# A 7x7 depthwise convolution on TensorE: from 32x4 output tiles with three products to paired 8x8 tiles with two products each

## The chip, the cores and the metric

The kernel runs on one core of one Trainium2 chip. The metric is the device time of one execution in microseconds, as the median of several runs. All data are float32. TensorE (PE) multiplies, with a separate weight-load stream (PEld); VectorE (DVE), ScalarE (ACT) and GpSimd (POOL) do the rest on chip; SyncE (SP), ACT and POOL also issue DMAs.

## The reference, cut to what matters

The input is an image `x` of 384 channels, 192 by 192. Layer 0 is a transposed-attention block: group norm, a 1x1 convolution to q, k and v with 2x2 max pooling, a 3x3 depthwise convolution, attention over channels, GELU, nearest upsampling and a projection; its output is added to `x`. Layer 1 is the stage that this change concerns:

```python
def _L1_conv_ref(x, weight):
    w_sym = (weight + rot90(weight, 1) + rot90(weight, 2) + rot90(weight, 3)) * 0.25
    return _dwconv(x, w_sym, 1, 3)      # 7x7, one filter per channel, padding 3

x = x + _L0_conv_ref(_gn(x), ...)       # layer 0
x = x + _L1_conv_ref(_gn(x), weight)    # layer 1; _gn: mean and variance over 12 channels
```

So the last stage normalises the image by group, convolves each channel with its own symmetrised 7x7 filter with zero padding, and adds the unnormalised image.

## The kernel before, in words

The kernel is one program whose stages follow each other: statistics of `x`; the q and k stage, in blocks of image rows (`products`, `pooled`, `depthwise`); the v stage with attention and projection (`convolve`, `depthwise_v`, `attend`, `project`, `residual`); and the 7x7 stage. Most of the order on each engine is written out by hand: `keep` pins an instruction to its program order.

**How a depthwise convolution becomes a product.** For one channel, an output tile of some rows and columns is a vector on the output partitions; the input window under it is a vector on the contracted partitions; the 7x7 filter, spread into a banded matrix, is the stationary operand; and all tiles of the image are the moving columns. Before, a tile is 32 rows (`TR`) by 4 columns (`CP`), 128 outputs, and the image has 6 by 48 = 288 such tiles (`NT`, `NJ`). The window of 38 rows by 10 columns does not fit into 128 partitions, so a channel takes three products of 288 columns: two from `main` (the tile's 32 rows, at two column shifts), and one from `aux`, which holds what is left over: three halo rows above, three below, and two columns of the tile's rows.

**Data in DRAM.** `residual` forms layer 0's result in an on-chip tile `sx` (POOL issues its stores) and writes it to `sd`, laid out by (column in tile, row in tile) so that a load gives `main` directly, and a second time, shifted, to `sh` for the halo rows. The spread filters are built on POOL during the q and k stage by `weights`, in 21 pieces, and written to `wt` (for `main`) and `wh` (for `aux`).

**The 7x7 stage** runs 48 steps of 8 channels (`CB`). In step n:

- ACT's queue issues the loads for step n+2 into three rotating buffers: `w` and `h` (weights), `main` and `aux` (data). The first two steps are loaded from SP's queue.
- POOL does `borders(n+1)`: it adds the mean outside the image (`mm`, `mb`), so that normalisation can be folded into weights and an offset row (`ONE`), and copies 32 rows of `main` into `aux`; then `spread(n-1)` reorders results into rows (`res`) and SP stores them.
- PE computes two channels into one of four PSUM tiles `pc` (`sums`). Each is drained, with the scale `rb`, by four instructions of 32 partitions by 576 elements into `apart`, on DVE and ACT in turn.
- After the second pair, `middle(n+1)` on DVE adds the identity (for the residual, scaled by `sb`) into the weights, and ACT copies the left-over rows (`rest`) and weight columns (`columns`) for step n+1.

Of the kernel before, what the change touches and what calls it, by code (L numbers as in the profile page):

```python
# [8 lines left out]
F32 = mybir.dt.float32  # L9
AF = mybir.ActivationFunctionType  # L10
ALU = mybir.AluOpType
AX = mybir.AxisListType

P = 128
# [47 lines left out]
CP = 4  # L62
NJ = HW // CP
JP = NJ + 2
RUN = NT * JP
HALO = KS // 2
NQ = CP + KS - 1
LEAD = JP + 2


TOP = 32
BOT = 64
ONE = TOP + HALO * NQ
REST = 96
SHR = REST - TOP
GQ = 3 * CP + 1
GR = 6
# [5 lines left out]
CB = 8  # L83


@with_exitstack
def conv_preact_d2(
# [27 lines left out]
    sd = dram.tile([CP * TR, C, RUN], F32, name="sd")  # L115

    sh = dram.tile([SHR, C, RUN], F32, name="sh")

    wt = dram.tile([P, C, 2 * P], F32, name="wt")
    wh = dram.tile([SHR, C, P], F32, name="wh")  # L120
# [143 lines left out]
    z = parkp.tile([P, RUN + 4 * P], F32, name="z")  # L264
    nc.vector.memset(z[:, 0:RUN], 1.0)
    nc.vector.memset(z[:, RUN:], 0.0)
# [338 lines left out]
    with ExitStack() as bx:  # L605
# [6 lines left out]
        def weights(kt, i0, i1):  # L612

            g = gwp.tile([P, GR, GQ, TR], F32, name=f"g{kt}_{i0}", tag="g")
            keep(nc.gpsimd.memset(g, 0.0))  # L620
            for kr in range(KS):
                lo, hi = max(i0, kr), min(i1, kr + TR)
                if lo < hi:
                    keep(nc.gpsimd.tensor_copy(
                        bass.AP(
                            g.tensor,
                            g.offset + ((lo - i0) * GQ + CP - 1) * TR + lo - kr,
                            [g.ap[0], [TR, KS], [GQ * TR + 1, hi - lo]],
                        ),
                        w7s[:, kt, kr, :].unsqueeze(2).to_broadcast([P, KS, hi - lo]),  # L630
                    ))
            yield
            lo, hi = max(i0, HALO), min(i1, HALO + TR)
            cs = slice(kt * P, (kt + 1) * P)
            for v in range(CP if lo < hi else 0):
                keep(nc.gpsimd.dma_start(
                    wt[v * TR + lo - HALO : v * TR + hi - HALO, cs].rearrange("f c n -> c f n"),
                    bass.AP(
                        g.tensor,
                        g.offset + ((lo - i0) * GQ + v) * TR,  # L640
                        [g.ap[0], [GQ * TR, hi - lo], [1, 2 * P]],
                    ),
                ))
            for i in range(i0, i1):
                if HALO <= i < HALO + TR:
                    continue
                f = i * NQ if i < HALO else BOT - TOP + (i - HALO - TR) * NQ
                keep(nc.gpsimd.dma_start(
                    wh[f : f + NQ, cs].rearrange("f c n -> c f n"),
                    bass.AP(  # L650
                        g.tensor,
                        g.offset + (i - i0) * GQ * TR,
                        [g.ap[0], [TR, NQ], [1, P]],
                    ),
                ))

        pieces = [
            (kt, i0, min(i0 + GR, TR + 2 * HALO))
            for kt in range(KT)
            for i0 in range(0, TR + 2 * HALO, GR)  # L660
        ]
        with tc.issue_after(loaded):
            for kt in range(KT):
                cs = slice(kt * P, (kt + 1) * P)
                for f in (ONE, BOT + HALO * NQ):
                    nc.sync.dma_start(
                        wh[f - TOP : f - TOP + 2, cs].rearrange("f c n -> c f n"),
                        z[:, RUN : RUN + 2 * P].rearrange("p (f n) -> p f n", f=2),
                    )
                    for k in range(2):  # L670
                        one = f + k == ONE
                        nc.sync.dma_start(
                            sh[f + k - TOP, cs], z[:, 0:RUN] if one else z[:, RUN : 2 * RUN]
                        )


# [93 lines left out]
        Q = 32  # L770

# [18 lines left out]
        def products(b, sides):  # L790
# [18 lines left out]
            grams, z[:, RUN : RUN + P], z[:, RUN : RUN + grams.shape[1]], start=True, stop=False,  # L809
# [154 lines left out]
        def weights_of(b):  # L964
            return weights(*pieces[b]) if b < len(pieces) else iter(())

# [76 lines left out]
        for b in range(2):  # L1043
# [25 lines left out]
            if b == 0:  # L1069
                with tc.issue_after(stats0):  # L1070
                    for _ in weights_of(b):
                        pass
# [37 lines left out]
        loose = iter(())  # L1110
# [8 lines left out]
        for n, (b, pair, half) in enumerate(groups):  # L1119
# [3 lines left out]
            if s == 0:  # L1123
                if b + 1 < NB:
                    xbs[b + 1] = load_x(b + 1, "xq")
                loose = weights_of(b - 1)
# [109 lines left out]
        early = gwp.tile([P, GR * GQ * TR], F32, name="vb_early", tag="g")  # L1236
# [195 lines left out]
    for i in range(3):  # L1432
        t = sxp.tile([P, LEAD + CP * RB * RUN + LEAD], F32, name=f"sx{i}")
        nc.gpsimd.memset(t, 0.0)
        sxs.append(t)

    junk = wq[:, 0:2, 0 : RB * NT * NJ].rearrange("p k (n j) -> p k n j", j=NJ)
# [21 lines left out]
    sdv = sd.rearrange("(v r) c n -> r c v n", v=CP)  # L1459
# [5 lines left out]
    def project(i, ot, gl, pin=lambda ins: ins):  # L1465
        b = order[i % NBC]
        y = yp.tile([P, NT, NJ, 2], F32, name=f"y{b}_{ot}", tag="y")
# [28 lines left out]
    def residual(i, ot, y, xr, pin):  # L1496
# [3 lines left out]
        xq = xr.rearrange("p t (a j e) -> p a t j e", a=RB, e=CP)  # L1500

        def at(e):

            return LEAD + (e + CP - 1) % CP * RB * RUN + int(e > 0)


        for e, f in ((1, 2), (0, 3)):
            for a in range(RB):
# [3 lines left out]
                            flat.tensor, flat.offset + at(e) + a * RUN,  # L1512
                            [flat.ap[0], [JP, NT], [1, NJ], [at(f) - at(e), 2]],
                        ),
                        xq[:, a, :, :, e : f + 1 : f - e],
# [12 lines left out]
        for k, (e, f) in enumerate(((1, 2), (3, 0))):  # L1528
            pin(
                nc.scalar.activation(  # L1530
                    junk,
                    bass.AP(
                        flat.tensor, flat.offset + at(e),
                        [flat.ap[0], [at(f) - at(e), 2], [JP, RB * NT], [1, NJ]],
                    ),
                    AF.Square, bias=negmid[:, ot : ot + 1], accum_out=sqsum[:, ot, b, k : k + 1],
                )
            )
            if k == 0:
                yield  # L1540
        cs = slice(ot * P, (ot + 1) * P)

        def rows_of(a, nv, shift):
            o = LEAD + a * RUN + shift
            return bass.AP(
                flat.tensor, flat.offset + o, [flat.ap[0], [RB * RUN, nv], [1, RUN]]
            )

        for a in range(RB):
            r = b * RB + a  # L1550
            nc.gpsimd.dma_start(sdv[r, cs], rows_of(a, CP, 0))  # L1551

            halos = []
            if r >= TR - HALO:
                halos.append(((r - TR + HALO) * NQ, -JP))
            if r < HALO:
                halos.append((BOT - TOP + r * NQ, JP))
            for h, shift in halos:
                for q in range(0, NQ, CP):
                    nv = min(CP, NQ - q)  # L1560
                    nc.gpsimd.dma_start(
                        sh[h + q : h + q + nv, cs].rearrange("f c n -> c f n"),
                        rows_of(a, nv, shift + q // CP),
                    )

# [71 lines left out]
    with ExitStack() as ex_:  # L1637

        fixed = ex_.enter_context(tc.tile_pool(name="fixed", bufs=1))
        wbufs = [fixed.tile([P, CB, 2 * P], F32, name=f"w_{i}") for i in range(3)]  # L1640
        early = ex_.enter_context(tc.tile_pool(name="early", bufs=1))
        hbufs = [early.tile([P, CB, P], F32, name=f"h_{i}") for i in range(3)]
        wide = ex_.enter_context(tc.tile_pool(name="wide", bufs=1))
        data = [P, CB, NT, JP]
        auxs, mainbufs = [
            [(wide if i > last else early).tile(data, F32, name=f"{name}{i}") for i in range(3)]
            for name, last in (("aux", 1), ("main", 0))
        ]
        outp = ex_.enter_context(tc.tile_pool(name="outp", bufs=2))

        CENTRE = (CP - 1) * TR
        eye = wide.tile([P, P], F32, name="eye")
        for k in range(CP):
            nc.gpsimd.tensor_copy(
                eye[:, k * TR : (k + 1) * TR], ident[:, (CP - 1 - k) * TR : (CP - k) * TR]
            )
# [10 lines left out]


        for h in hbufs:
            nc.gpsimd.memset(h[0:TR, :, 2 * TR :], 0.0)  # L1670
            nc.gpsimd.memset(h[REST:P, :, TR:], 0.0)

        def load_w(n):
            w = wbufs[n % len(wbufs)]
            queue(n)(w, wt[:, span(n)])
            return w

        def load_h(n):
            h = hbufs[n % len(hbufs)]
            queue(n)(h[TOP:REST], wh[:, span(n)])  # L1680
            return h

        def columns(n):

            k = 2 * TR
            w, h = ws[n]
            keep(nc.scalar.copy(h[0:TR, :, 0 : 2 * TR], w[k : k + TR, :, 6 * TR :]))
# [328 lines left out]
```

## Time and profile before

| | |
|---|---|
| median of 3 runs | 2701.74 us (2700.86 to 2702.03) |
| profiled execution, time | 2689.47 us |
| its span | 2687.8 us |
| mean granted TensorE clock | 0.986 |
| 7x7 stage, first to last product | 2109.6 to 2677.0 us |
| busy over the span: PE, DVE, ACT, POOL | 93%, 84%, 53%, 54% |

The profile is one execution, whose own time is 12.3 us under the median of the other runs; durations are taken from it. A group's row names the line of the kernel, the engine, the operation, output and inputs, and shape and count; then busy time, mean length of one, and idle time of the engine before them with what ended it. PE's instructions overlap, so their spacing is read from starts and not from lengths; an f32 product shows as two instructions, each with a weight load.

### The profile page before, as it was taken

Reading aid. Unit: us, or ns where it says so; the run is one execution under the profiler, and the core shown is the slowest. Engines: PE = TensorE matmul, PEld = TensorE weight load, DVE = VectorE, ACT = ScalarE, POOL = GpSimd, SP = SyncE. Lnnn points to the kernel's source line nnn. Section 1 sums busy time; section 2 is a strip of 40 time slices with the busy share of each in tenths; the row PEclk is TensorE's granted clock in tenths of the full one; section 3 lists DMA queues with packets and bytes.
Section 4 is the critical chain, followed back from the end, with each engine's and each line's share of the span. In section 5 each row is a group of like instructions: output and inputs, shape, how many; then the busy total and the mean of one; then the engine's idle time right before and its main releaser. Section 6 shows DMA issues by size and latency. Waiting matters only on the chain. (4 is left out here: it accounts for less than half of the span.)

```text
span 2687.8 us, 29574 instructions
## 1 busy us (share of the span) xinstructions
PE 2509.0 (93%) x8893; PEld 1628.8 (61%) x8893; DVE 2270.1 (84%) x3172; ACT 1420.9 (53%) x2711; POOL 1462.9 (54%) x1587
## 2 busy tenths in 40 slices
PE   0298999999999999999899999999999799999998
PEld 0144565656565656565565666666666577777776
DVE  7986788888888888878699989998888788899887
ACT  0032667676767676776213223222234677777776
POOL 1013788888887988876212311001011677878876
PEclk9999999999999999999899999999999899999999
DMA  9962354546363645443428997657657999999998
GB/s 378 399 248 53 106 177 118 157 117 189 109 191 84 181 124 170 131 119 70 127 89 307 387 359 234 230 180 255 208 164 249 339 352 360 374 367 372 363 380 255
DMA packets 467630, 609.59 MB, mean 227 GB/s; under 512 B 250224, under 2 KB 399312, under 8 KB 450704
## 3 DMA queue, kind: packets, MB, share of 16 engines
q1 hardware_dynamic: 407104, 311.83, 37.0%
q0 software_dynamic: 37344, 148.84, 15.4%
q10 hardware_dynamic: 23024, 147.05, 14.6%
q8 instruction: 71, 1.16, 0.2%
q14 instruction: 87, 0.71, 0.1%
HBM read 370.93 MB, written 208.21 MB: 215 GB/s over the span
## 5 line engine op out<-in xcount | busy, mean ns | idle before, releaser
L563 PE MATMUL pv<-xv,wq 128*128 128x384 f32 x1512 | 498.0, 490 | 13.9 <-DVE rows L569 6.2
L1920 PE MATMUL pc<-main,w 128*128 128x288 f32 x1536 | 435.3, 406 | 4.0 <-POOL aux L1840 1.2
L563 PEld LDWEIGHTS pv<-xv,wq 128*128 128x128 f32 x1512 | 289.1, 192 | 214.3 <-DVE rows L569 6.9
L1940 DVE TENSOR_SCALAR apart<-pc,rb 32x576 f32<-32x576 f32 x384 | 312.2, 813 | 75.2 <-PE pc L1920 56.0
L897 POOL TENSOR_TENSOR qk<-qk,more 128x384 f32<-128x384 f32 x290 | 309.7, 1074 | 109.9 <-ACT more L896 100.9
L1938 ACT ACTIVATE apart<-pc,rb 32x576 f32<-32x576 f32 x384 | 281.4, 733 | 132.2 <-PE pc L1920 127.5
L1920 PEld LDWEIGHTS pc<-main,w 128*128 128x128 f32 x1536 | 289.3, 189 | 89.0 <-PE pc L1920 3.9
L1551 POOL DMA_DIRECT2D sd<-sx x96 | 72.4, 757 | 493.0 <-DVE sx L1510 474.4
L596 DVE SCALAR_TENSOR_TENSOR vb<-rows,wd,vb 128x576 f32<-128x576 f32 x360 | 293.8, 818 | 10.7
L897 POOL TENSOR_TENSOR qk<-qk,rows 128x384 f32<-128x384 f32 x216 | 230.5, 1072 | 76.2 <-ACT rows L896 69.9
L1920 PE MATMUL pc<-aux,h 128*128 128x288 f32 x768 | 248.6, 406 | 0.7 <-POOL main L1828 0.4
L929 DVE SCALAR_TENSOR_TENSOR bank_r<-ring,wd,bank_r 128x384 f32<-128x384 f32 x383 | 236.4, 617 | 6.8
L1879 POOL COPY res<-apart 128x1152 f32<-128x1152 f32 (+1 forms) x96 | 223.5, 2355 | 11.5 <-ACT apart L1938 6.2
L1037 PE MATMUL bank_b<-rows,more 128*128 128x384 f32 x528 | 220.4, 499 | 2.0 <-ACT bank_c L1139 1.2
L1510 DVE TENSOR_TENSOR sx<-xr,y 128x576 f32<-128x576 f32 x180 | 203.9, 1173 | 18.1 <-ACT y L1481 15.1
L1117 DVE TENSOR_TENSOR rows<-bank_c,rows 128x384 f32<-128x384 f32 x132 | 73.3, 555 | 126.7 <-PE bank_c L1037 68.6
L569 DVE TENSOR_REDUCE rows<-pv 128x192 f32<-128x768 f32 x144 | 137.6, 956 | 49.8 <-PE pv L563 49.8
L1763 DVE SCALAR_TENSOR_TENSOR w<-eye,sb,w 128x512 f32<-128x512 f32 x96 | 175.9, 1871 | 1.5
L1530 ACT ACTIVATE wq<-sx,negmid 128x1152 f32<-128x1152 f32 x96 | 120.6, 1256 | 102.6 <-DVE sx L1510 100.4
L1920 PEld LDWEIGHTS pc<-aux,h 128*128 128x128 f32 x768 | 144.5, 189 | 43.6 <-POOL main L1828 2.5
L896 ACT ACTIVATE more<-ring,wd 128x384 f32<-128x384 f32 x290 | 170.3, 608 | 0.0
L1456 ACT ACTIVATE gl<-po 128x288 f32<-128x288 f32 x96 | 39.5, 411 | 225.2 <-PE po L1449 225.2
(349 smaller groups left out, 4934.7 us busy)
## 6 DMA issues: line engine op xcount, KB each, us to landing
sd<-sx POOLq DMA_DIRECT2D x96, 600.0 KB, 9.9
out_dram<-res SPq DMA_DIRECT2D x192, 288.0 KB, 11.0
main<-sd ACTq DMA_DIRECT2D x46, 1200.0 KB, 6.7
xr<-in_x_dram SPq DMA_DIRECT2D x45, 1152.0 KB, 12.3
xq<-in_x_dram SPq DMA_DIRECT2D x21, 2304.0 KB, 8.6
xv<-in_x_dram SPq DMA_DIRECT2D x126, 384.0 KB, 7.3
w<-wt ACTq DMA_DIRECT2D x46, 1024.0 KB, 7.2
xs<-in_x_dram SPq DMA_DIRECT2D x24, 1536.0 KB, 15.2
```

The costliest lines, as they stand in the source:

```text
L563: nc.tensor.matmul(ps[:, u, 0 : RB * HW], wq[:, kt, o : o + P], xb[:, u, kt, :], start=(kt == 0), stop=(kt == KT - 1),)
L596: pin(nc.vector.scalar_tensor_tensor(dst, src, w, dst, ALU.mult, ALU.add))
L896: keep(nc.scalar.mul(part.rearrange("p (h w) -> p h w", w=PS), src, w))
L897: keep(nc.gpsimd.tensor_tensor(flat, flat, part, ALU.add))
L929: nc.vector.scalar_tensor_tensor(into, src, w, before, ALU.mult, ALU.add)
L1037: nc.tensor.matmul(ps[:, 0:HN], lhs, rhs, start=start, stop=True, skip_group_check=True)
L1510: nc.vector.tensor_tensor(bass.AP(flat.tensor, flat.offset + at(e) + a * RUN, [flat.ap[0], [JP, NT], [1, NJ], [at(f) - at(e), 2]],), xq[:, ...
L1763: nc.vector.scalar_tensor_tensor(mid, eye.unsqueeze(1).to_broadcast([P, 4, P]), sb[:, c : c + 1], mid, ALU.mult, ALU.add,)
L1879: keep(copy(res[ps, k], apart[ps, :, k].rearrange("p e n -> p n e")))
L1920: nc.tensor.matmul(ahead[q][:, k, 0 : NT * NJ], lhs, rhs, start=(j == 0), stop=(j == 2), skip_group_check=True,)
L1938: keep(nc.scalar.mul(dst, src, scale))
L1940: keep(nc.vector.tensor_scalar_mul(dst, src, scale))
```

## The change

A tile becomes 8 rows by 8 columns (`ED`), 64 outputs; the image has 24 by 24 = 576 of them, in two halves of 288. The window is 14 rows by 16 columns, taken as two products of 14 rows by 8 columns at two column shifts, plus an offset row. For each channel and shift, one half of the tiles goes to PSUM partitions 0 to 63 and the other to 64 to 127, with the same 64-column weights: four products per channel. There is no `aux`, no `h`, no `sh` and no `wh`.

- `main` has 25 slots (`SLOTS`) of 25 tiles. Two DMAs of 32 partitions load eight image rows per slot; `below` copies the lower rows of the window on chip from the slots of the next strip: 32 partitions on POOL, 24 on ACT, two instructions each.
- `borders` works on the two loaded 32-partition blocks only: the two end columns, and one slot above and one below the image.
- A PSUM tile of two channels is drained by one instruction of 128 partitions by 576 elements, three of four on ACT, the fourth on DVE. `apart` now collects 16 channels.
- `swapped` turns results with VectorE's 32x32 transposes, six of 768 elements per 16 channels, one after each drain of the next two steps; `stored` writes runs of four image rows, 24 DMAs per 16 channels.
- `middle` adds into four places of 128 elements instead of two of 512, on 96 partitions.
- `weights` builds three tiles instead of 21 pieces; each is written by 28 DMAs in runs of 64 elements. `residual` writes eight column phases: four DMAs of 150 to 175 element runs per row pair and channel tile, and no halo copies.

The core of the diff:

```diff
-CP = 4
-NJ = HW // CP
-JP = NJ + 2
-RUN = NT * JP
+ED = 8
+NJ = HW // ED
+JP = NJ + 1
+STRIPS = NT * JP
+SLOTS = 4 * NT + 1
+RUN = SLOTS * JP
...
-    sd = dram.tile([CP * TR, C, RUN], F32, name="sd")
-    sh = dram.tile([SHR, C, RUN], F32, name="sh")
-    wt = dram.tile([P, C, 2 * P], F32, name="wt")
-    wh = dram.tile([SHR, C, P], F32, name="wh")
+    sd = dram.tile([ED * ED, C, RUN], F32, name="sd")
+    wt = dram.tile([2, P, C, ED * ED], F32, name="wt")
...
         def load_main(n):
             main = mainbufs[n % len(mainbufs)]
-            queue(n)(main.rearrange("p c t j -> p c (t j)"), sd[:, span(n)])
+            for k in range(2):
+                queue(n)(
+                    main[2 * k * Q : (2 * k + 1) * Q].rearrange("p c t j -> p c (t j)"),
+                    sd[k * Q : (k + 1) * Q, span(n)],
+                )
             return main
...
+        def below(n, copy, base, rows, cs=slice(0, CB)):
+            main = mains[n]
+            to = main[base + Q : base + Q + rows, cs].rearrange("p c t j -> p c (t j)")
+            src = main[base : base + rows, cs].rearrange("p c t j -> p c (t j)")
+            keep(copy(to[:, :, 0 : 2 * STRIPS], src[:, :, STRIPS : 3 * STRIPS]))
...
+        def swapped(n, apart):
+            res = outp.tile([P, NT, RQ, HW], F32, name=f"res{n}", tag="res")
+            for k in range(NT):
+                keep(
+                    nc.vector.transpose(
+                        res[:, k].rearrange("p r (j q) -> p j r q", q=ED)[:, :, ::-1],
+                        apart[:, k].rearrange("p c (s j) -> p j (c s)", j=NJ),
+                    )
+                )
+                if k % 3 == 2:
+                    stored(n, res, k // 3)
+                yield
...
+            for q in range(CB // 2):
+                ps = pc.tile([P, 2, 512], F32, name=f"pc{n}_{q}", tag="pc")
                 for k in range(2):
                     i = 2 * q + k
+                    for j in range(2):
+                        rows = ONE + 1 - j
+                        for h in range(2):
+                            keep(
+                                nc.tensor.matmul(
+                                    ps[h * 2 * Q : (h + 1) * 2 * Q, k, 0 : 2 * NT * NJ],
+                                    w[0:rows, j, i],
+                                    main[0:rows, i, 2 * NT * h : 2 * NT * (h + 1), j : j + NJ],
+                                    start=(j == 0), stop=(j == 1), skip_group_check=True,
+                                )
                             )
...
+                if q == 3:
+                    keep(nc.vector.tensor_scalar_mul(dst, src, rb[:, c : c + 1]))
+                else:
+                    keep(nc.scalar.mul(dst, src, rb[:, c : c + 1]))
+                next(swapping, None)
+                if q == 0 and n + 1 < steps:
                     middle(n + 1)
+                    below(n + 1, nc.scalar.copy, 2 * Q, KS * ED - Q)
```

## The prediction

> **What bounds the kernel now.** I first read the table by stretches of time, because the edit concerns one stage. Its columns are the stretch, its length, then busy time and instruction count of PE, PEld, DVE, ACT and POOL, the granted clock, the DMA share and GB/s.
>
> ```profile
> 2000.00:2100.00 100.00, 81.49 (x309) 59.95 (x307) 87.79 (x109) 51.59 (x114) 19.82 (x30) 0.90 0.68 238
> 2300.00:2400.00 100.00, 99.65 (x411) 77.13 (x410) 86.99 (x86) 77.03 (x95) 78.40 (x78) 1.00 1.02 368
> ```
>
> Inside the 7x7 stage (second line) TensorE never stops and the DMA engines are full as well; the other three engines run at 77 to 87%. The groups (busy us, mean ns of one, idle before) give the price list:
>
> ```profile
> L1920 PE MATMUL pc<-main,w 128*128 128x288 f32 x1536 | 435.3, 406 | 4.0 <-POOL aux L1840 1.2 <-issue 1.1 <-POOL main L1828 0.9
> L1940 DVE TENSOR_SCALAR apart<-pc,rb 32x576 f32<-32x576 f32 x384 | 312.2, 813 | 75.2 <-PE pc L1920 56.0 <-POOL aux L1840 6.8 <-POOL aux L1848 6.8
> L1938 ACT ACTIVATE apart<-pc,rb 32x576 f32<-32x576 f32 x384 | 281.4, 733 | 132.2 <-PE pc L1920 127.5
> L1867 ACT COPY aux<-main 32x2304 f32<-32x2304 f32 x48 | 101.7, 2119 | 0.6
> L1840 POOL COPY aux<-main 32x2304 f32<-32x2304 f32 x48 | 101.0, 2104 | 3.0
> ```
>
> PE waits 4 us in all for the stage's main products, while DVE and ACT wait for PE: PE is the bound. Its pace is read from the timeline (start, length, count), at the same place in two successive channels:
>
> ```profile
> 2305.50 0.65 PE L1920 MATMUL pc<-aux,h 128*128 128x288 f32 x2
> 2306.96 0.65 PE L1920 MATMUL pc<-aux,h 128*128 128x288 f32 x2
> ```
>
> 1.46 us for a channel of three products. Each f32 product is two instructions, so a slot is 1.455/6 = 242.5 ns; the 406 ns is the length of one instruction, overlapping the next. A step of 8 channels is 11.64 us, 48 steps 559 us. The stage's products run from 2109.6 to 2677.0 us: 567 us, 11.82 a step.
>
> How near DMA is to taking over is seen in its queues over 2200 to 2500 us (packets, MB, share) and in a wait:
>
> ```profile
> q10 hardware_dynamic: 11527, 81.11, 72.1%
> q1 hardware_dynamic: 39176, 28.89, 29.2%
> POOL main L1828 <- DMA main<-sd: 86.0, 38, 4.9
> ```
>
> q10 (loads) moves 81.11/(0.721 x 300) = 375 GB/s while it has the engines, q1 (stores in 768-byte runs) 330. The loads come just in time, so bytes matter as much as products.
>
> [...] LDWEIGHTS time goes by columns. [...] 163 ns for 96 columns, 190 for 128. [...] min/median/max below, where the minimum fell beside an idle POOL. [...]
>
> ```profile
> L1763 DVE SCALAR_TENSOR_TENSOR w<-eye,sb,w x96: 736/2080/2739, 2107.2 to 2662.2; 128x512 f32<-128x512 f32 x96
> ```
>
> Two more rows of the trace before price operations that the change adds: the transposes of an earlier stage (same columns), and a run of weight loads with tiny products (a row of the groups by shape).
>
> ```profile
> L861 DVE STREAM_TRANSPOSE turns<-qk x144: 534/578/579, 202.8 to 1296.7; 128x384 f32<-128x384 f32 x144
> ```
>
> ```profile
> L489 PEld LDWEIGHTS bank_y<-mean,wq 128*128 128x128 f32 x54 | 6.3, 192 | 0.5 <-issue 0.5
> ```
>
> **The change part by part, per step of 8 channels.**
>
> PE: three products of 128 output columns become four of 64, in two column halves, all with 288 moving columns. In program order each half issues its two passes (h0 h0 h1 h1 h0 ...). A half's second pass waits for its first, but can run beside the other half's first, so a steady stream has two in flight: 8 instructions in 4 slots, 0.97 us a channel, 7.76 us a step. Without overlap: 8 slots, 15.52 us. Issue allows it: in the L489 row 54 weight loads with their one-column products take 6.3 us, 117 ns a pair, so two pairs need at most 234 of a slot's 242 ns.
>
> ACT: three drains of 576 elements per partition (733 each, whatever the partitions) = 2.20; two lower-row copies of 2400 elements, by L1867 2.2 each = 4.4; three DMA issues (before, 0.34 for w and a median of 0.61 for main) = 1.5. Sum 8.1 us. Gone are five drains, the L1867 copy, the two h copies and two issues.
>
> POOL: two border additions of 400 elements; from L1828 (325 ns at 48, 395 at 96) 1.46 ns an element, 0.84 each; two row copies of 200, 0.35 each (L1855: 507 for 384); two lower-row copies at L1840's rate, 2.2 each. Sum 6.8 us. The res copies (two of 2358) and the aux work go.
>
> DVE: one drain 0.81; four additions into w of 128 elements, 736 less 384 elements at 1.04 ns = 0.34 each, 1.4; three transposes of 768 elements, from L861's 578 at 384 0.98 each, 2.9. Sum 5.1 us. [...] median less minimum of L1763 is 1.34 us; if each of the four pays that, 10.5 us.
>
> SP: 12 stores instead of 4, each issue 0.316 us by the old ones: 3.8 us. It runs nothing else there.
>
> DMA: loads fall from 1200+1024+600+256 KB to 1250 (64 of 128 rows are loaded, the rest copied) + 512 KB, 1.80 MB; stores stay 1.18 MB, in runs of 3072 bytes. At 375 GB/s for both, 7.9 us; at the 398 GB/s seen from 70 to 135 us with long runs, 7.5. [...]
>
> The buffer ring is the last term. A main buffer's load is queued on ACT when the products three steps back end (about 1 us), lands in 6.7 to 15.2 us (say 8.5), then borders 2.4, copies 4.4, products 7.8: 24.1 us over three buffers, 8.0 a step; at 10.5 us landing 8.7.
>
> New waits: ACT's lower-row copies wait for POOL's border work on the same buffer, and behind them in ACT's queue stand two drains and the next step's DMA issues; the additions into w can wait for POOL on DVE, with a transpose and the fourth drain behind, which PE needs four PSUM tiles later; SP's stores wait for transposes, with only stores behind them.
>
> Five resources thus lie between 6.8 and 8.1 us with little slack, and they wait for one another, ACT's late DMA issue above all. I take 8.6 us; bounds 8.0 (ACT, DMA) and 10.5. So 48 x 8.6 = 413 against 567: **-154 us**.
>
> Stage ends. Start: the first product waits for borders, then 600-element copies (0.75 us each) for two channels only, and 1800-element ones for the rest; the last stores of ot 0 take four POOL issues of 0.75 instead of two before main can load. Removed: h memsets 3.7 us on POOL, hidden. I take +4 (0 to +8). End: after the last drain six transposes (5.9) and 12 issues (3.8) stand where 2.2 us copies and four issues stood: +4 (+2 to +7).
>
> Earlier stages. The padding-weight building drops 21 memsets of 2.2 us and about 130 small copies from POOL for three of each; its DMAs stay near 80 at about 0.9 us but in 256-byte runs. PE is 99.8% busy there (600 to 900 us), so 0; if slower packets delay loads, +5. In the projection stage 192 stores to sd replace 96 and the 54 halo stores, 72+40 us of issue becoming 145 on POOL, which is 9 to 16% busy: 0. The residual addition (L1510, 1172 ns for 576) gets other strides; I keep its price. Bounds 0.97 and 1.36 us; only the 45 at the stage's DVE-bound end (first line above: DVE 88, PE 81) lie on the path, -9 to +9.
>
> Sum: -154 + 4 + 4 = -146. The profiled execution took 2689.5 us (span 2687.8); the median of three is 2701.7, 12 above it. Carried over: **2556 us**.
>
> **Rivals.**
> A. The halves do not overlap (f32 passes, or weight loads into the other half held back). Then 15.52 us a step, 745 + 9 against 567, plus 8: about 2896, slower. It decides once a channel's eight instructions need more than 1.48 us, 6.1 slots, i.e. under half the possible overlap. For it: nothing here shows two tiles at once. Against: [...] L489's issue pace.
> B. [...] four short additions behind 2.2 us POOL copies, 10.5 us a step: 504 - 567 + 8 = -55, 2647. For: L1763's median. Against: POOL is idle a fifth of the time[...].
> C. [...] For: POOL already waits 86 us for main. Against: stores run between.
>
> **How the numbers follow.** Forecast (8.0 to 10 us a step) 0.62: own range 2515 to 2625. B and C together 0.18: 2600 to 2700. A, whole or mostly, 0.18: above 2707. No change 0.02; about 0.2% (5 us) is what this measurement can tell. Faster 0.80, slower 0.18. The range 2510 to 2720 leaves out A and a little below.
>
> **What would show it.** PE's products in pairs a few ns apart and 7.8 to 8.6 us a step; busy ACT near 6.6 us a step, POOL near 6.8; transposes near 0.98 us; DMA still near full at 30% fewer bytes. Starts 242 ns apart, never together, mean A; additions into w of over 1.3 us with PE waiting for DVE mean B; main landing after 10 us or more with POOL waiting for it mean C.

## The result, and the profile after

The changed kernel takes 2881.4 us (median of 4; before 2701.9 in the same comparison): **1.0665 times the time before, 95% interval 1.0646 to 1.0683**. The forecast was faster.

The table by stretches (columns as before: length, then PE, PEld, DVE, ACT, POOL, granted clock, DMA share, GB/s) now reads:

```profile
2000.00:2100.00 100.00, 74.16 (x291) 54.56 (x290) 79.90 (x89) 50.03 (x112) 34.71 (x48) 0.88 0.90 195
2300.00:2400.00 100.00, 65.59 (x405) 37.95 (x404) 73.42 (x51) 43.98 (x34) 45.07 (x41) 0.84 0.77 195
```

In the 7x7 stage (second line) nothing is full any more: PE 66%, DVE 73%, ACT and POOL under half, DMA 0.77 at 195 GB/s where it was 1.02 at 368. Engines that all have slack in a stage that got longer point to waits of engines for one another. The stage's products run from 2132.4 to 2851.1 us: 15.0 us a step against 11.8. Of the 190 us between the two profiled spans, 152 are the stage, 23 its later start, 15 what follows the last product.

The groups of the page give the prices to set beside the forecast's (busy, mean ns | idle before, what ended most of it):

```profile
L1848 PE MATMUL pc<-main,w 120*64 120x288 f32 (+1 forms) x3072 | 503.9, 475 | 222.1 <-ACT main L1779 120.0
L1814 DVE STREAM_TRANSPOSE res<-apart 128x768 f32<-128x768 f32 x144 | 293.4, 2061 | 117.5 <-DMA main<-sd 44.4
L1862 ACT ACTIVATE apart<-pc,rb 128x576 f32<-128x576 f32 x144 | 101.5, 738 | 413.4 <-DMA out_dram<-res 139.4
L1761 POOL TENSOR_TENSOR main<-main,mm 32x400 f32<-32x400 f32 x95 | 88.1, 928 | 392.0 <-DMA main<-sd 341.2
L1694 DVE SCALAR_TENSOR_TENSOR w<-eye,sb,w 96x128 f32<-96x128 f32 x192 | 221.8, 1212 | 5.7 <-DMA w<-wt 5.7
```

PE, which before waited under 5 us for its products in all (4.0 for those from `main`, 0.7 for those from `aux`), waits 222; a transpose takes 2061 ns where 980 were forecast; drains and border additions cost what was forecast. The odd entry is the third: ACT's **drain**, which needs only PE's products and a free buffer, waits for the landing of a **store**. One step on the timeline shows how (start, length, engine, count, idle before and its end):

```profile
2398.28 0.38 ACTq L1624 DMA_DIRECT2D w<-wt  x1
...
2398.71 7.84 ACTq L1624 DMA_DIRECT2D main<-sd  x2
...
2406.65 0.74 ACT L1862 ACTIVATE apart<-pc,rb 128x576 f32<-128x576 f32 x1 [9.19 <-DMA out_dram<-res]
...
2407.41 2.20 ACT L1779 COPY main<-main 24x2400 f32<-24x2400 f32 x1
...
2409.52 2.19 ACT L1782 COPY main<-main 24x2400 f32<-24x2400 f32 x1
2409.71 0.67 PE L1848 MATMUL pc<-main,w 121*64 121x288 f32 x2 [3.05 <-ACT main L1779]
```

ACT's queue issues three loads for a later step. The first issue takes 0.4 us; the pair after it 7.8, since the second of the pair is held. Behind it, in ACT's order, stand a drain and both lower-row copies, and for these copies PE waits. What holds the issue is seen in the semaphores of the trace, on which it records waits and landings. SP's and ACT's DMAs share eight, in turn: each of the eight has 222 or 223 of the 1780, and from 2180 to 2640 us SP's 360 stores leave out 90 places of the turn, as many as ACT issues loads. An issue waits until the DMA eight places earlier has landed: on the four semaphores whose landings the trace has in full, each of 886 issues ends 0.33 us or more after that landing. Here the second load of `main` goes out at 2406.21 us, 0.07 us after the landing, at 2406.14, of a store that SP had issued at 2400.31 on the same semaphore. Before, a step had four stores and four loads, so a load always met the semaphore of an older load (ACT's loads stand on four of the eight, SP's stores on the other four). Now it has twelve stores and three loads, and a load meets a store's, or that of the weight load issued just ahead. The stores in turn wait for the slow transposes (last line below). The waits between 2135 us and the end sum it up (engine, line waited for, us, times, longest):

```profile
POOL main L1761 <- DMA main<-sd: 324.5, 75, 10.2
...
ACT apart L1862 <- DMA out_dram<-res: 139.4, 15, 10.3
ACT apart L1862 <- DMA w<-wt: 133.2, 15, 9.8
PE pc L1848 <- ACT main L1779: 120.0, 34, 6.6
...
SPq L1798 <- DVE res L1814: 232.5, 71, 25.6
```

The DMA queues over 2200 to 2500 us (packets, MB, share) show a second loss:

```profile
q10 hardware_dynamic: 7328, 35.77, 47.9%
q1 hardware_dynamic: 11237, 23.02, 30.2%
```

Loads move 35.77/(0.479 x 300) = 249 GB/s while they hold the engines, against 375 before. A 20000-byte packet of `main` takes a median of 1407 ns in the trace after 2135 us, 14.2 GB/s an engine.

Finally, rival A named nearly this time (2896), but not for its reason. One step's products, on the timeline of PE:

```profile
2304.33 7.98 PE L1848 MATMUL pc<-main,w 121*64 121x288 f32 x62 [1.47 <-ACT main L1782]
```

These are 62 of the step's 64 instructions, two a product (the first two ran at 2302.19 us, ahead of a wait), with a median length of 406 ns. Their starts follow one another by some 40 and some 205 ns in turn, so a pair takes 0.243 us and 64 take 7.8, as forecast. In series they would need 15.5. At 2302.19 us the two instructions of one product, alone on PE, start 265 ns apart; at 2304.33 one of each half start 7 ns apart. The halves do overlap; PE then stands idle, and the mean granted clock of the stretch is 0.84 where it was 1.00. That clock costs too: an instruction took 406 ns at the median where the granted clock was 1.0, and 687 where it was 0.5. Over the whole stage the mean is 475 ns, and PE is busy 10.5 us a step at a mean clock of 0.83, where f15 below has 410 ns and 8.1 us at 0.99. How much of the longer stage is this clock and how much the waits, no run separates.

### The profile page after: what moved, and what is told of

It is laid out like the page before. It is cut to its first block, busy times and chain, and to the rows that moved or that the text cites. A ratio compares the mean times of both kernels' runs of the same rounds, so it can differ in the third digit from the quotient of the medians.

```text
span 2877.7 us, 30797 instructions
## 1 busy us (share of the span) xinstructions
PE 2443.9 (85%) x9661; PEld 1497.1 (52%) x9661; DVE 2303.8 (80%) x3068; ACT 1294.4 (45%) x2424; POOL 1317.6 (46%) x1329
## 3 DMA queue, kind: packets, MB, share of 16 engines
q10 hardware_dynamic: 19344, 84.97, 11.9%
## 5 line engine op out<-in xcount | busy, mean ns | idle before, releaser
L1848 PE MATMUL pc<-main,w 120*64 120x288 f32 (+1 forms) x3072 | 503.9, 475 | 222.1 <-ACT main L1779 120.0
L1848 PEld LDWEIGHTS pc<-main,w 120*64 120x64 f32 (+1 forms) x3072 | 304.6, 160 | 420.7 <-issue 282.3
L1512 POOL DMA_DIRECT2D sd<-sx x192 | 143.9, 753 | 540.4 <-DVE sx L1475 497.3
L1814 DVE STREAM_TRANSPOSE res<-apart 128x768 f32<-128x768 f32 x144 | 293.4, 2061 | 117.5 <-DMA main<-sd 44.4
L599 DVE SCALAR_TENSOR_TENSOR vb<-rows,wd,vb 128x576 f32<-128x576 f32 x360 | 293.6, 817 | 10.6
L1862 ACT ACTIVATE apart<-pc,rb 128x576 f32<-128x576 f32 x144 | 101.5, 738 | 413.4 <-DMA out_dram<-res 139.4
L1761 POOL TENSOR_TENSOR main<-main,mm 32x400 f32<-32x400 f32 x95 | 88.1, 928 | 392.0 <-DMA main<-sd 341.2
L1694 DVE SCALAR_TENSOR_TENSOR w<-eye,sb,w 96x128 f32<-96x128 f32 x192 | 221.8, 1212 | 5.7 <-DMA w<-wt 5.7
L1010 PE MATMUL bank_x<-xq,wq 128*128 128x384 f32 x378 | 154.7, 491 | 1.0 <-ACT bank_b L1062 1.0
L1010 PE MATMUL bank_y<-xq,wq 128*128 128x384 f32 x378 | 155.0, 492 | 0.0
L1444 PE MATMUL pr<-gl,wp 128*128 128x288 f32 x576 | 142.6, 406 | 0.0
## 6 DMA issues: line engine op xcount, KB each, us to landing
xs<-in_x_dram SPq DMA_DIRECT2D x24, 1536.0 KB, 15.5
```

The source lines that it names most:

```text
L599: pin(nc.vector.scalar_tensor_tensor(dst, src, w, dst, ALU.mult, ALU.add))
L1010: nc.tensor.matmul(ps[:, 0:HN], lhs, rhs, start=start, stop=True, skip_group_check=True)
L1444: nc.tensor.matmul(ps[:, 0:H], wp[:, ct, ot * P : (ot + 1) * P], gl[:, ct, h * H : (h + 1) * H], start=(ct == 0), stop=(ct == KT - 1),)
L1512: nc.gpsimd.dma_start(sdv[r + a, cs, RQ - e : ED - e, o : o + n], bass.AP(flat.tensor, flat.offset + JP + (a * ED + e) * STRIPS - (e > 0) ...
L1694: nc.vector.scalar_tensor_tensor(mid, eye[0 : 3 * Q, k].rearrange("p r q -> p (r q)").unsqueeze(1).to_broadcast([3 * Q, 4, ED * RQ]), sb[0 ...
L1814: nc.vector.transpose(res[:, k].rearrange("p r (j q) -> p j r q", q=ED)[:, :, ::-1], apart[:, k].rearrange("p c (s j) -> p j (c s)", j=NJ),)
```

## The experiments

Three suspects from the trace: **S**, the loads' semaphores are coupled to the stores'; **T**, the transposes take 2.06 us; **L**, loads of 32 partitions run at two thirds of the old rate. Per kernel: ratio to before, us a step from first to last product start, and us from the last product start to the end of the span.

| kernel | edit against the change | ratio (95%) | a step | end |
|---|---|---|---|---|
| before | | 1 | 11.8 | 11 |
| after | | 1.0665 (1.0646-1.0683) | 15.0 | 27 |
| e2_flat | T out | 1.0394 (1.0342-1.0446) | 13.8 | 24 |
| e3_swload | S out | 1.0107 (1.0070-1.0143) | 11.9 | 32 |
| e4_mid | one load of 64 partitions | 1.0053 (1.0040-1.0066) | 11.8 | 25 |
| e12_mid_two | same place, two loads of 32 | 1.0693 (1.0672-1.0713) | 15.0 | 27 |
| e5_mid_sw | S, L out | 0.9919 (0.9904-0.9934) | 10.6 | 33 |
| e9_mid_sw_flat | S, L, T out | 0.9868 (0.9840-0.9896) | 10.3 | 37 |
| e11_mid_sw_po | S, L, T out, result in order | 0.9863 (0.9842-0.9883) | 10.1 | 37 |
| f13_po_r3 | e11, three result buffers | 0.9837 (0.9805-0.9869) | 9.8 | 53 |
| f14_po_half | e11, stores of half the bytes | 0.9690 (0.9657-0.9723) | 9.4 | 38 |
| f15_po_six | e11, half the stores | 0.9467 (0.9439-0.9496) | 8.6 | 13 |
| f16_po_r3_last | f13, other queues at the end | 0.9797 (0.9768-0.9825) | 9.9 | 41 |
| g17_big_sw | S, L, T out, 6 larger stores a step | 0.9528 (0.9504-0.9552) | 9.0 | 24 |
| g18_big_act | g17, loads on ACT's queue | 0.9631 (0.9616-0.9647) | 9.5 | 24 |

**What makes a transpose slow.** Two of three transposes were changed, one in what it reads, one in what it writes:

```diff
+ if k % 3 == 1:   # contiguous input
+     at = apart[:, k].rearrange("p c n -> p (c n)").rearrange("p (j m) -> p j m", m=Q)
+ if k % 3 == 2:   # contiguous output
+     to = res[:, k].rearrange("p r n -> p (r n)").rearrange("p (j m) -> p j m", m=Q)
```

> Leaves the order of results in two thirds of the tiles wrong: of the six transposes of each buffer, two stand as in the change (strided in, strided out), two read apart contiguously and write strided, two read strided and write contiguously. It prices the access pattern. If the strided read is what makes 2.06 us of the 0.98 that was forecast, the group with contiguous reads falls to about 1.0 us and the group with contiguous writes stays near 2.0; if the write does, the other way round; if the price goes with the 768 elements or the 24 blocks of 32x32 alone, all three stay at 2.0 to 2.1. The span should fall by no more than 100 us; under the theory of the coupled loads alone it stays within 20 us of 2878.

The row of the transposes (min/median/max ns):

```profile
L1819 DVE STREAM_TRANSPOSE res<-apart x144: 924/2042/2092, 2150.0 to 2839.3; 128x768 f32<-128x768 f32 x144
```

Split by place in the program, the means are 2073 ns as in the change, 947 with contiguous reads, 2052 with contiguous writes. The **read** order makes the price: results that the transpose takes one after the other lie 24 results (96 bytes) apart. One time of this kernel, 2858 us.

> Leaves the results in the wrong order within each tile: all transposes read and write contiguously; nothing else differs. Theory T (the transposes are late, and the stores and through the shared DMA semaphores the loads with them): the transpose falls to 1.0 us or less, the stage of 15.0 us a step falls by 3 us or more a step, total 2700 to 2740. Theory S (loads are coupled to the stores by the rotation of eight semaphores, whatever the transposes take): the wait of ACT's apart on stores shrinks, but the second half of main is still issued 6 us late or more; total 2800 to 2860. Theory L (loads of 32 partitions at 14 GB/s an engine bound the stage): total above 2830.

With all reads contiguous: 2815 us, transposes of 964 ns. T is real, worth 0.027, but the stage keeps 13.8 us a step. That is the range named for S, not the one for T.

**The coupling.** Edit: `engine = nc.sync if n < 2 else nc.gpsimd` in `queue`, so that loads take POOL's queue and its own semaphores (in the change POOL's 285 DMAs stand on eight others, 35 or 36 on each). The edit also takes their issues out of ACT's order.

> The loads of w and main from the third step on are issued by POOL's queue, which has semaphores of its own; stores stay on SP's, transposes stay at 2.06 us. Theory S: ACT's waits on landings of out_dram and w (139 + 133 us) go, the drains and lower-row copies run on time, the stage falls to what DVE takes, 12 to 13 us a step, total 2740 to 2800. Theory T: DVE is then busy throughout at some 12 us a step or more, and the total is above 2780. Theory L: the waits move to POOL's copies of main, which wait for landings; total above 2840. [...]

2737 us, just below the range named for S. The waits after 2135 us now begin:

```profile
ACT apart L1862 <- PE pc L1848: 195.3, 58, 12.0
POOL w L1624 <- PE pc L1848: 123.5, 17, 14.8
DVE res L1814 <- DMA out_dram<-res: 91.2, 12, 11.7
```

The drains wait for PE and no longer for landings; POOL waits 7 us for `main` where it waited 324. The packets of `main` still take a median of 1332 ns, so nearly all of the gain of 0.056 came without faster loads. That a landing held the issue is read in the trace of the change (0.07 us, above); how much of the gain is the uncoupling and how much the free ACT queue, this run doesn't part. Issuing the loads later in ACT's order, or with more semaphores, was not tried.

**One load in place of two.** `main`'s two loaded blocks are put side by side at partitions 32 to 95 and fetched by one DMA; the copied rows go to 0 to 31 and 96 to 119:

```diff
-            for k in range(2):
-                queue(n)(main[2 * k * Q : (2 * k + 1) * Q]..., sd[k * Q : (k + 1) * Q, span(n)])
+            queue(n)(main[Q : 3 * Q]..., sd[:, span(n)])
```

> The two loaded blocks of main lie side by side at partitions 32 to 95 and come in one DMA of 64 partitions; the copied lower rows lie at 0 to 31 and 96 to 119. Transposes and queues stay as in the change, but a step has 2 loads in place of 3, so the rotation of eight semaphores comes in 14 transfers a step in place of 15. Theory L: packets of 20000 bytes fall from 1405 ns to 800 to 1000 ns, DMA's share in the stage from 0.78 to about 0.6, total 2740 to 2820. Theory S: the coupling stays but no second half is queued behind the first; total 2800 to 2870. Theory T alone: within 20 us of 2881.

2718 us, below the range named for L, and packets with a median of 746 ns (mean 929); DMA's share did not fall as expected (0.79 over 2400 to 2500 us), since more steps pass in the same time. That alone leaves open whether the place, the single transfer or the shorter rotation helped. The same place with two loads of 32 partitions:

> The two loaded blocks of main lie side by side at partitions 32 to 95, but still come in two loads of 32 partitions each, on ACT's queue: 15 transfers a step in the rotation of eight semaphores, as in the change. It splits the 164 us that one load of 64 brought. If those were the number of loads (the second one queued behind a landing): 2860 to 2890 as in the change. If they were the part of the partitions that the loads go to: 2710 to 2760, with packets of 20000 bytes well below 1400 ns.

2876 us, the range named for the number of loads, and packets with a median of 1418 ns. So the place does nothing; one transfer of 64 partitions does. For `main` an engine moves 14.2 GB/s in the change (20000 B / 1407 ns) and 26.8 with the load of 64 (20000 B / 746 ns); what in the wider transfer makes its packets faster, no run here shows. The number of loads changed with their rate, so these two kernels don't part rate from coupling; the next one does.

> Both of the last two edits: main comes as one load of 64 partitions, and the loads are issued by POOL's queue. DVE keeps transposes of 2.06 us. [...] this gains on both: 2640 to 2690, with DVE busy over 85% of the stage and its transposes (6.2 us a step), additions (4 to 5) and drain (0.8) as the bound, 11 to 12 us a step. If they are two ways of curing one thing, late loads, it stays at 2700 to 2730.

2665 us, in the range named for two separate losses. With loads on POOL's queue in both, the one load of 64 brings 0.019 (e3 to e5; it also spares POOL one issue a step). On ACT's queue it brought 0.061. The 0.042 between them go with the second issue in the shared rotation, most likely with its being held; a rotation of 14 in place of 15 changed with it.

**What transposes cost after that.** The same with contiguous transposes:

> One load of 64 partitions on POOL's queue (2665 with strided transposes), and transposes that read and write contiguously, which leaves the results in the wrong order within each tile; the stores are those of the change. It takes 3.3 us a step from DVE, which in the 2665 us kernel was busy for 89% of the stage. If DVE bounds that kernel: the stage falls from 11.2 to 9 to 9.7 us a step, where POOL (6.8 + 2 issues of 1 us) or ACT (6.6) stands next, total 2560 to 2600. If something else bounds it: 2640 or more.

2655 us: only 0.005 less. That is not the 2560 to 2600 of a stage bound by DVE, but the other range (2640 or more), in which something else bounds it. DVE's busy share fell from 0.89 to 0.55 over 2200 to 2600 us and hardly anything followed. The end grew to 37 us. Something named by none of the three stood next.

Three kernels sought the same with the right order of results, by letting the drain write `apart` in the transposes' order. The block of 32 then holds first 16 channels of one tile row, then of the other, and the stores follow:

```diff
-                [[HW * HW, CO], [TR * HW, 2], [1, RQ * HW]],
+                [[TR * HW, 2], [HW * HW, CO], [1, RQ * HW]],
```

> One load of 64 partitions, issued by ACT's queue as in the change; and the drains write apart in the order in which the transposes read it, so that each block of 32 is contiguous (the read order was what made 2.06 us). The result is the reference's. Transposes should take 0.95 to 1.0 us; the drains, which now write single elements 64 bytes apart, 0.74 to 1.3 us. If the transposes were on the path through the coupled stores: 2620 to 2680. If the coupling itself holds (a load waits for the store eight transfers before it): above 2680.

> Loads on POOL's queue and transposes that read contiguously; main still comes as two loads of 32 partitions. [...] If the load rate of 14 to 15 GB/s an engine bounds the stage once nothing else does: DMA share of 0.95 or more, 11 us a step, total 2680 to 2720. If not: 2600 to 2660.

> All three edits at once; the result is the reference's. The three terms that the forecast had wrong are taken away, so the stage should come near the forecast's 8.6 us a step, but with two DMA issues of 1 us more on POOL (6.8 + 2 = 8.8) [...]: 9 to 10 us a step, 2126 + 48 x 9.5 + 15 = 2590 to 2620. If it stays above 2660, something that none of the three names bounds the stage.

3453, 3553 and 3423 us, ratios 1.286, 1.322 and 1.274: far above every range named, and all three have the diff above. The third kernel between 2200 and 2900 us, in its waits:

```profile
DVE res L1813 <- DMA out_dram<-res: 517.6, 13, 41.4
```

While only stores run (3350 to 3400 us), its DMA share is 0.13 and the rate 52 GB/s. Their stores have an outer dimension of 2, those of the change 16. A share of 0.13 is what two of 16 engines would give (0.125); that only two worked is an estimate from this share. These three runs say nothing of S, T and L.

Two ways to get the order with stores as in the change, both by changing the order of results in PSUM:

> As the last, but with the reference's result: the products read main with the tile row innermost, so that the two results that belong side by side in a transposed block come side by side in PSUM, and the drains write apart in runs of four results. Stores keep an outer dimension of 16 (the runs with an outer dimension of 2 had 52 GB/s in their stores, against 277). If the products keep 0.24 us a pair and the drains 0.75 us: 2570 to 2620. If the strided reading slows the products, or the short runs the drains (1.2 us in the last two kernels): up to 2680.

> The same order of results in PSUM, but made by the side that writes: the products read main as in the change and write PSUM with a stride of 12 results. Same numbers: 2570 to 2620 if product and drain keep their times; if writing with a stride slows the products, above 2680. Which of the two is free is not known beforehand.

Reading `main` with a stride doubles an instruction's time, from 406 to 797 ns (first kernel, ratio 1.1482, 19.6 us a step):

```profile
L1847 PE MATMUL pc<-main,w 120*64 120x288 f32 x656 | 252.8, 797 | 0.0
```

Writing PSUM with a stride costs nothing (second kernel: median 406 ns), and gives 2652 us, the same as e9, with DVE at 0.56. Both miss 2570 to 2620; the first also exceeds the 2680 named for slow reading.

**The stores.** At its end the second kernel (e11) issues stores alone (timeline of SP: start, length, count):

```profile
2587.66 59.25 SPq L1797 DMA_DIRECT2D out_dram<-res  x85
```

The same for the kernel with half the bytes in each store (f14, below):

```profile
2579.53 35.66 SPq L1797 DMA_DIRECT2D out_dram<-res  x56
```

0.70 and 0.64 us a store. With full bytes and a third result buffer (f13, below) the end shows 0.64 as well, so the pace there hardly depends on the bytes. Within the stage the same kernel issues 450 stores in 400 us, 0.89 us each: twelve take 10.7 us where a step takes 9.8, and a backlog grows.

```profile
2602.71 51.44 SPq L1797 DMA_DIRECT2D out_dram<-res  x80
```

```profile
L1797 SPq DMA_DIRECT2D out_dram<-res x450: 549/592/2432, 2199.7 to 2599.5; - x150
```

The issue itself (min/median/max, 2200 to 2600 us), in the kernel before and after:

```profile
L1883 SPq DMA_DIRECT2D out_dram<-res x136: 315/316/2777, 2204.6 to 2597.4; - x136
```

```profile
L1798 SPq DMA_DIRECT2D out_dram<-res x315: 550/591/3163, 2199.5 to 2599.8; - x158
```

So an issue of a store takes 0.59 us where the older form took 0.316; what in its form sets this was not tested. And SP's queue waited for landings already in the kernel before (its waits over the same stretch: 111 times for an earlier store):

```profile
SPq L1883 <- DMA out_dram<-res: 193.2, 111, 8.2
```

> The 2652 us kernel (one load of 64 partitions, loads on POOL's queue, products that write PSUM strided) with three result buffers in place of two. If DVE's waits for stores (125 us in 400) are a matter of buffers: they go, the stage falls to 9 us a step, total 2600 to 2625. If the stores' rate is the bound: the backlog only moves to the end, the tail grows from 37 to 50 us or more, total 2640 to 2655.

> The 2652 us kernel; each of the 576 stores writes only the first half of its bytes (1536 in place of 3072 a packet), so half of the results are not stored. If the number of stores bounds (issue of 0.59 us, eight in flight): total 2630 to 2652, SP's pace of 0.69 us a store at the end unchanged. If the bytes on the DMA engines bound: 2580 to 2610, stage near 9 us a step.

> The 2652 us kernel with 288 stores of full size in place of 576; the other half of the results are not stored. Same bytes as the kernel with half packets. If the number bounds: 2570 to 2600, with a tail under 15 us and DVE's waits for stores gone. If the bytes bound: the same as the kernel with half packets, within 10 us. If neither does: 2635 to 2652.

> Three result buffers, and the last 24 stores are issued by ACT's and POOL's queues, which are idle by then, 12 each; the result is the reference's. If the end is SP's queue alone (0.69 us a store): the tail falls by 15 to 20 us against the kernel with three buffers on SP's queue alone. If the DMA engines or the transposes set the end: by less than 5 us.

A third buffer moves the backlog to the end (53 us): rate, not buffers. Half the bytes bring 0.017 (e11 to f14). Half the number at those same bytes brings 0.022 more (f14 to f15; the packets are halved too), both together 0.040, with an end of 13 us. Number and bytes thus weigh about alike here; g17 below, which stores all bytes in half the stores, is 0.034 below e11, with other edits in it. The half-bytes kernel landed between its two ranges; half the number fell below its own. Its stage is the one that was forecast (timeline of PE, and its stretch):

```profile
2303.01 8.02 PE L1847 MATMUL pc<-main,w 121*64 121x288 f32 x64 [0.40 <-POOL main L1781]
2311.48 8.02 PE L1847 MATMUL pc<-main,w 121*64 121x288 f32 x64 [0.45 <-POOL main L1781]
2319.89 8.03 PE L1847 MATMUL pc<-main,w 121*64 121x288 f32 x64 [0.39 <-POOL main L1781]
```

```profile
2200.00:2500.00 300.00, 283.39 (x2263) 158.14 (x2264) 199.72 (x284) 226.16 (x179) 287.86 (x285) 1.00 0.84 283
```

64 instructions every 8.4 to 8.5 us, each step released by POOL's last copy; POOL, with the loads' issues, is busy 96%. Other queues for the last 24 stores cut the end by 12 us, not 15 to 20: ACT's twelve were issued only at 2630.7 us, 27 us after the last product, and the first of them waits in the trace for a semaphore that a store of SP's backlog held. That was not tested by itself.

**The whole result in few stores.** Collecting 32 channels makes the transposed partitions channels alone, so one store takes two tile rows:

```diff
-  for kk in range(3 * k, 3 * k + 3):     # 24 DMAs of 96 KB per 16 channels
-      [[HW * HW, CO], [TR * HW, 2], [1, RQ * HW]]
+  # per two tile rows: 24 DMAs of 192 KB per 32 channels
+      [[HW * HW, Q], [TR * HW, 2], [1, RQ * HW]]
```

> Results are collected over four steps (32 channels) in place of two, so that the transposed partitions are channels alone and one store takes two tile rows: 288 stores of 192 KB in place of 576 of 96 KB, all results stored. The drains write apart with the channel innermost, the transposes read contiguously, main comes as one load of 64 partitions, loads on POOL's queue. If the number was what held the stage: 8.6 to 9.0 us a step, total 2560 to 2590 (a tail of 20 to 25 us, since twelve transposes and four steps' bytes are left at the end). If the bytes hold it: 9.5 us a step or more, 2610 to 2640. The drains write single results 128 bytes apart; at the 1.2 us that such drains took earlier ACT would need 8.1 us a step.

> As the last, with the loads on ACT's queue as in the change. A step then has eight transfers, six stores and two loads, in the rotation of eight. If the coupling needs only a shared rotation: ACT waits for stores as in the change, total 30 us or more above the kernel with loads on POOL's queue. If it needs stores that are late: within 15 us of it, or less, since POOL, the busiest engine, loses its two issues (1.3 us a step).

**g17 is the best version: 2584 us, 0.9528 of before**, in its range, with 9.0 us a step:

```profile
2200.00:2500.00 300.00, 276.25 (x2162) 164.62 (x2158) 236.51 (x269) 218.47 (x169) 274.57 (x269) 0.99 0.96 337
```

PE and POOL at 92%, DMA share 0.96: three resources near full, as the forecast had meant. With its loads on ACT's queue (g18) it is 29 us slower, just short of the 30 named for a shared rotation. ACT then waits for PE (112 us over 2200 to 2600) and not for stores. POOL waits for `main`, and SP's stores now wait for landings of loads, the coupling in reverse (g17 has no such wait):

```profile
POOL main L1759 <- DMA main<-sd: 86.6, 33, 5.6
```

```profile
SPq L1796 <- DMA main<-sd: 60.1, 10, 7.0
```

So a shared rotation still costs with eight transfers a step, but a fraction of what it cost with fifteen; how much of the 29 us is rotation and how much the ACT issue time was not separated.

## Why the prediction was wrong, step by step

- **PE, right in mechanism.** 7.76 us a step in two overlapping halves; 7.8 measured at full clock. That the halves overlap was the author's estimate: no product before shows two at once. The forecast had no term for a lower clock, and over the stage PE was busy 10.5 us a step. Rival A's mechanism is refuted by the after timeline and again by 8.6 us a step in f15, though its time was nearest.
- **ACT, POOL: prices right.** Drains 0.738 (0.733 taken), copies 2.19 (2.2), border additions 0.93 (0.84). Wrong was the **1.5 us for three DMA issues**: an issue was priced as its own length, and it can be held.
- **The step that failed first** is the sentence "SP's stores wait for transposes, with only stores behind them", and with it, in the buffer ring, that a load "is queued on ACT when the products three steps back end (about 1 us)". Behind the stores stood, through the rotation of eight, the loads, and behind those ACT's drains and copies. Loads on a queue of their own gave back 0.056 (e3), a single load on the old queue 0.061 (e4), more than any other single edit of the change.
- **SP, mis-sized and wrongly hidden.** 12 x 0.316 = 3.8 us; an issue takes 0.59, and with its waits a store takes 0.64 to 0.70 at the end and 0.89 within the stage (f13), so 12 take 7.7 to 10.7. The wait on landings (193 us) stood in the trace before and was not read. Half the stores gave 0.022 at equal bytes (f14 to f15).
- **Transposes, mis-sized.** 0.98 us from L861's row; 2.06 measured. The row shows shapes, not the order in which they are read. Worth 0.027 alone (e2), 0.005 once S and L were gone (e5 to e9).
- **DMA.** The 32-row loads are slow: 249 GB/s for the load queue, where the forecast took 375 to 398; no load before shows what 32 rows cost. Rival C (loads bind; its times were an estimate that no trace showed) was partly right in mechanism (POOL waits 324 us for `main`) but put the landing at 10 us or more; it is 6.1 after an issue that is late. The rate alone is 0.019 (e3 to e5).
- **Additions into w.** Range 0.34 to 1.68 each; 1.21 the mean measured (median 0.48, longest 2.32). 90 of the 192 took over 1 us, and these ended 0.14 to 0.15 us after a POOL instruction did, as 72 of the 96 before had, 0.55 to 0.56 us after one; what ties the two engines was not shown. Not the bound that rival B made of them.
- **Start, +23 instead of +4.** Read in the trace, not tested: the last residual addition ends at 2100.7 instead of 2096.4 us, while POOL's issues to `sd` wait for landings (18.4 us from 2060 to 2106); the first load of `main` is issued at 2104.4 instead of 2094.2, behind a DMA of ones into buffers that `sx` still held; and a first load then takes up to 23.6 us to land, at most 15.2 before. **End, +15 instead of +4**: mostly stores at SP's pace; it is 13 us in all with half the stores (f15), but still 24 with fast transposes (e2).
- **The sum.** The losses aren't additive: S alone brings 0.056, the single load 0.061, both 0.075. With all of them gone and half the stores left out the stage took 8.62 us a step for a forecast of 8.6. That match is partly luck: there POOL, with the loads' issues, is the bound at 96%, and half the results are not stored. The range ended at 2720 because each wait was bounded by itself, and none by what stood behind it in another engine's queue.

## What to carry to other kernels

When a change alters the number of DMAs per step, count them per step and queue, and ask which earlier DMA each must wait for, before pricing any as hidden; the wait may then stand in an engine's instruction order and stop work that has nothing to do with it. Price an operation from a row with the same access order, not only the same shape (here 0.95 and 2.06 us for one shape). When all engines have slack after a change that cut everyone's work, look in the waits for an engine that waits for something it doesn't use.

## What the hardware showed that was not expected

- A DVE 32x32 transpose of 768 elements: 0.95 us reading contiguously, 2.06 reading elements 96 bytes apart; writing strided costs nothing (947 ns in e1 with strided writes, 964 in e2 with contiguous ones).
- An instruction of a product of 288 f32 columns: 406 ns, 799 when the moving operand is read 100 bytes apart (e10), 406 when PSUM is written 48 bytes apart (e11).
- An ACT drain of 576 results: 0.74 us, 1.25 when it writes single results 768 bytes apart (e8), 0.76 when it writes pairs (g17).
- Stores whose outer dimension is 2 moved 52 GB/s while only they ran (e8).
